# A decoder layer on one core: the feed-forward weights split before the value products, in other memory

## The chip, the core and the metric

The kernel runs on one core of a Trainium2 chip. Its work is done by TensorE (matmuls, PE in the profile, with the weight loads as PEld), VectorE (DVE), ScalarE (ACT) and GpSimd (POOL); SyncE (SP) issues the DMAs. The metric is the time of one execution in microseconds, as the median of several runs. One further execution is profiled; its own time stands beside its span.

## The reference

A post-norm decoder layer over `x` of 8 sequences of 128 tokens and 512 features:

```python
x = layernorm(x + attn(x))            # 32 query heads, 8 key/value heads of 128, int4 weights with scales, rope, causal
x = layernorm(x + xattn(x, ctx))      # 16 heads of 32; softmax over axis 0 (batch and heads)
x = layernorm(x + ffn(x))

def xattn(q, v, k):
    Q, K, V = (proj(t, W, b) for t, W, b in ((q, Wq, bq), (k, Wk, bk), (v, Wv, bv)))
    scores = einsum('bqd,bkd->bqk', Q, K) / sqrt(32)
    return einsum('bqk,bkd->bqd', softmax(scores, axis=0), V)      # heads put back as (d, head)

def ffn(x):                            # 8 experts, top 2, rank 16
    gates = relu(layernorm_affine(x @ gw1.T + gb1)) @ gw2.T + gb2
    w = ...                            # softmax of the top two, zero for experts over their capacity
    return x @ weight.T + einsum('enr,ero->no', einsum('ni,eir->enr', x, lora_A) * w.T[:, :, None], lora_B) / 16
```

## The kernel before

Products that need full fp32 accuracy are made of fp32r parts: an operand is rounded to a high part (a cast on ScalarE), the low part is the difference (a subtraction on VectorE or POOL), and three matmuls (high-high, high-low, low-high) are summed in PSUM. VectorE, ScalarE, POOL and TensorE each execute their instructions in the order in which the kernel writes them; SyncE's order is made by the framework.

The first 500 us are the self-attention. Then a string, `ORDER` (L57), sets the order of the second stage, one letter per step: among them `Q` (one of eight query products of the cross-attention, `queries`), `B` (score products), `M` and `E` (maxima and exponentials), `s` and `S` (sums of exponentials on POOL, L1038 to L1044; the last one is added up on TensorE, L1136), `z`, `Z` (the softmax denominator on TensorE, L1078) and `V` (a quarter of a value projection, L682, with the copy of the result at L687). Here `V` with `pxv` multiplies context parts by the split weights Wv. The scaled softmax factors are in `gmax`.

After `ORDER` the feed-forward weights `fw` (four pieces of 128x512) are loaded (L1161), the gate's small constants are made (`gate_constants`: memsets of `rank`, `ones`, `minus_one`, `places` and a row of `hT` on POOL, L1190 to L1198, and two VectorE instructions on `order`, L1196 and L1197, that read `rank`), and the identity is added to the weights' four diagonal blocks on POOL (L1205): that adds the residual to the product.

The third stage goes by sequences, i = 0 to 7. Strings `AV_FIRST` (i = 0 and 1, L79) and `AV_SEQ` give the order within a step: `A` value products with the probabilities (`cross_values`: TensorE `xav` L1384, copy to `avs` L1393), `B` transposes and residual (`cross_residual`: `tr_av` L1398, VectorE L1400, statistics with `rstd_x` and `nmr_x` on POOL at L252 and L254), `L` the normalisation of the previous sequence on ScalarE (L255), `X` its transposes with high and low parts `x2h`, `x2l` (`turn_x2`: L1240 to L1242), `P` the gate product `pg` (L1247), `f` one quarter of the queued work: first value projections, later the feed-forward product `pf` of the sequence before (L1261, three matmuls), and `W` one of four weighings of sequence i + 2: exponentials times factor and inverse denominator (L1234), on VectorE for three and on POOL for one (`WEIGH_ON`). With `B` of i = 1 come the late inverses (L1225 to L1227).

The split of the feed-forward weights lies in step i = 1, as letters `s` and `t`, since its memory is that of the split weights Wv, which the last value projection reads at the start of that step (`o`, `open_parts`):

```python
def split_weights(*kts):
    for kt in kts:
        nc.scalar.copy(fw_parts["h"][:, kt, :], fw[:, kt, :])
        nc.gpsimd.tensor_tensor(fw_parts["l"][:, kt, :], fw[:, kt, :], f32(fw_parts["h"][:, kt, :]), ALU.subtract)
```

A pool `fw` holds four rows (tag `raw`), used for `avs` and later for five of the eight output tiles `o`. The last stage (`END_SEQ`) finishes the gate, adds the experts' part and normalises.

Of the kernel before, what the change touches and what calls it, by code (L numbers as in the profile page):

```python
# [10 lines left out]
F32 = mybir.dt.float32  # L11
F32R = mybir.dt.float32r
# [41 lines left out]

ORDER = (  # L57
    'WXOOWXOOXAOKOTAAXOWOKTLKLKAOOTOOKWLOOTOOKLKXXQXKBKMAQKKKEBATQMLEKKVsAXVBAVTSsVQVTMSTLVEBVLNsLSQM'
    'EVBNQsVMEVBNVQSsSMgEVBQVNVsMEBVShMNsEVVVyVzSVZVVVV'
)  # L60
AV_SEQ = 'ALHfBNEJWWhhGffXKkfkPMWW'
GATES = ((0, 4, 'av'), (4, 2, 'sc'), (6, 1, 'po'), (7, 1, 'tr'))
# [13 lines left out]
SUB = (2, 3, 4, 5, 6)  # L76
TAIL = 8
TAIL_FIRST = 4
AV_FIRST = ('ALfBWWffWfW', 'AfLBffWWfoXsPWtW')  # L79
SEQUENCE = 'TpOpApOVpOpOp'  # L80
OUT_LANES = ('out0', 'out1')
TINY = 1e-25
# [51 lines left out]
def f32(ap):  # L134
    return ap.bitcast(F32)
# [3 lines left out]
def decoder_kernel(ctx: ExitStack, tc: tile.TileContext, a: dict, out: bass.AP):  # L139
# [37 lines left out]
    def pool(name, side="left", bufs=1):  # L177
        cm = tc.tile_pool(name=name, bufs=bufs, side=side)
        return cm, cm.__enter__()

    def close(cm):
        cm.__exit__(None, None, None)
# [889 lines left out]
    def sum_of(terms, first=True, last=True):  # L1072
# [4 lines left out]
        for i, x in enumerate(terms):  # L1077
            nc.tensor.matmul(ps[:], ident[:], x, start=first and i == 0, stop=last and i == len(terms) - 1)  # L1078

    last_terms = late_sum = None  # L1080
    for what in ORDER:
        n = count_of[what] = count_of.get(what, -1) + 1
        tick()
        if what == "O":
            outs.pop(0)()
            if not outs:
                flush()
                psum["ready"] += LANES.values()
        elif what == "K":
            late.pop(0)()  # L1090
        elif what == "V":
            open_exponentials()
            fill.pop(0)()
        elif what == "X":
            assert n < HALF or not outs
            norms.append(turn_out(n))
        elif what == "A":
            norms.pop(0)()
        elif what == "T":
            tokens.append(turn_x1(n))  # L1100
        elif what == "L":
            tokens.pop(0)()
        elif what == "Q":
            queries(n)
        elif what == "B":
            products(n)
        elif what == "M":
            if n == 0:
                open_maximum()
            group_maximum(n)  # L1110
        elif what == "W":
            wq_lows.pop(0)()
        elif what == "z":
            sum_of(last_terms[: 2 * HALF], last=False)
        elif what == "Z":
            nc.vector.tensor_tensor(gsum[:, 0, :], lsum[0][:], factor[:, 0, :], ALU.mult)
            nc.vector.tensor_tensor(gsum[:, 1, :], late_sum[:], factor[:, 1, :], ALU.mult)
            give(lsum[0], late_sum)
            sum_of(last_terms[2 * HALF :], first=False)
        elif what == "N":  # L1120
            last_chunk(SUB[n])
        elif what == "s":
            first_sum(n)
        elif what == "E":
            if n < GROUPS - 1:
                exponentials(n, range(3 if n in SUB else 4))
            else:
                last_terms = last_exponentials()
        elif what == "S":
            if n < EARLY:  # L1130
                group_sum(n)
            else:
                part = parts.pop(n)
                late_sum = bank("sum", "gsum6", (P, S))
                for i in range(HALF):
                    nc.tensor.matmul(late_sum[:], ident[:], part[:, i, :], start=(i == 0), stop=(i == HALF - 1))  # L1136
        elif what == "g":

            nc.gpsimd.tensor_tensor(
                gmax[:, early, :], gmax[:, early, :], across(gmax[:, EARLY - 1, :], EARLY - 1), ALU.subtract  # L1140
            )
            nc.scalar.activation(gmax[:, early, :], gmax[:, early, :], AF.Exp, scale=xscale)
        elif what == "h":
            nc.gpsimd.tensor_tensor(gsum[:, early, :], gsum[:, early, :], gmax[:, early, :], ALU.mult)
        elif what == "y":
            sum_of([gsum[:, i, :] for i in range(EARLY)])
    assert not (outs or late or norms or tokens or burst) and len(fill) == TAIL
    nc.vector.tensor_tensor(gmax[:, :KT, :], gmax[:, :KT, :], across(factor[:, 0, :], KT), ALU.mult)
    close(sub_cm)
    close(query_cm)  # L1150


    fw_cm, fwp = pool("fw", "right")
    fw = context_pool.tile([P, KT, D], F32, tag="ch", name="fw", bufs=2)
    fw_parts, x2 = {}, {}
    small = context_pool.tile([P, KT, D], F32, tag="cl", name="fg_lb", bufs=2)[:].rearrange("p k n -> p (k n)")
    fg = small[:, : KT * (FW - D)].rearrange("p (k c) -> p k c", k=KT)
    lb = small[:, KT * (FW - D) : KT * (FW - D) + D]

    for kt in range(KT):  # L1160
        nc.sync.dma_start(fw[:, kt, :], a["fw"][ts(kt, P), :D])  # L1161
    nc.sync.dma_start(fg, a["fw"][:, D:].rearrange("(k p) c -> p k c", p=P))
    nc.sync.dma_start(lb, a["loraB"])

# [33 lines left out]
        nc.gpsimd.memset(hT[GH : GH + 1], 1.0)  # L1198

    f_cm = open_ffn()  # L1200
    gate_constants()

    for kt in range(KT):
        diagonal = fw[:, kt, ts(kt, P)]
        nc.gpsimd.tensor_tensor(diagonal, diagonal, ident[:], ALU.add)  # L1205

    def split_weights(*kts):
        for kt in kts:
            nc.scalar.copy(fw_parts["h"][:, kt, :], fw[:, kt, :])
            nc.gpsimd.tensor_tensor(fw_parts["l"][:, kt, :], fw[:, kt, :], f32(fw_parts["h"][:, kt, :]), ALU.subtract)  # L1210


    inverse = gmax[:, GROUPS - 1, :]
# [152 lines left out]
    def engine_of(m, on=WEIGH_ON):  # L1366
        return nc.vector if on[m] == "v" else nc.gpsimd
# [10 lines left out]
    def cross_values(i):  # L1378

        av = bank("sc", f"xav{i}", (P, KT, S))  # L1380
        hf, j = divmod(i, HALF)
        for k in range(XH):
            m, g = divmod(k, 4)
            nc.tensor.matmul(  # L1384
                av[ts(g, XD), m, :],
                values_of(i)[:, ts(k, XD)],
                scores_of(4 * (hf * KT + m) + g)[:, j, :],
                start=True,
                stop=True,
                tile_position=(0, g * XD),  # L1390
            )
        avs[i] = fwp.tile([P, KT, S], F32, tag="raw", name=f"avs{i}", bufs=KT)
        nc.scalar.copy(avs[i][:], av[:])  # L1393

    def cross_residual(i):
        tr = bank("po", f"tr_av{i}", (P, KT, S))
# [24 lines left out]
    def step(what, i, state):  # L1421
        if what == "L" and i - 1 in apply:
            apply.pop(i - 1)()
        elif what == "W" and i + 2 < B:
            m = state["w"] = state.get("w", -1) + 1
            weigh(i + 2, m, engine_of(m))
        elif what == "A" and i < B:
            cross_values(i)
        elif what == "B" and i < B:
            cross_residual(i)  # L1430
            if i == 0:
                weigh(1, KT - 1, nc.vector)
            elif i == 1:
                late_inverses()
        elif what == "X" and i:
            turn_x2(i - 1)
        elif what == "P" and i:
            norm[i - 1] = gate_in(i - 1)
        elif what == "N" and norm:
            norm.pop(min(norm))()  # L1440
        elif (what == "G" and i == GATE_IN) or (what in "Hh" and i == GATE_IN + 1):
            gate(0, what)
        elif what == "M" and i == B - 1:
            apply.pop(i)()
        elif what == "k" and i == B - 1:
            gate(1, "h")
        elif what in "JK" and i == B - 1:
            gate(1, "GH"["JK".index(what)])
        elif what == "E" and i in EVACUATE:
            evacuate(EVACUATE.index(i))  # L1450
        elif what == "f" and fill:
            fill.pop(0)()
        elif what == "o":
            assert not fill
            open_parts()
        elif what in "st":
            split_weights(*((0, 1), (2, 3))["st".index(what)])

    def open_parts():

        fw_parts.update({m: xk["work"].tile([P, KT, D], F32R, tag=f"xwv{m}", name=f"fw{m}") for m in "hl"})
        x2.update({m: xk["work"].tile([P, HALF, KT, S], F32R, tag=f"c{m}1", name=f"x2{m}") for m in "hl"})

    rest = fill[TAIL_FIRST:]
# [65 lines left out]
    def finish(n):  # L1530
# [12 lines left out]
            aggregations.pop(0)()  # L1543

        if n % 3 == 0:
            o = fp.tile([P, D], F32, tag="x2f", name=f"o{t}", bufs=3)
        else:
            o = fwp.tile([P, D], F32, tag="raw", name=f"o{t}", bufs=KT)
        nmr = stat.tile([P, 1], F32, tag="nmr", name=f"nmr{t}")
        if APPLY_ON[n] == "p":  # L1550
            mine.append(lambda: nc.gpsimd.tensor_scalar(nmr[:], mv[:, 0:1], rstd[:], -1.0, ALU.mult, ALU.mult))
# [1 line left out]

        def apply():
            if APPLY_ON[n] == "v":
                nc.vector.tensor_scalar(o[:], y, mv[:, 0:1], rstd[:], ALU.subtract, ALU.mult)
            else:
                if APPLY_ON[n] == "a":
                    nc.vector.tensor_scalar(nmr[:], mv[:, 0:1], rstd[:], -1.0, ALU.mult, ALU.mult)
                nc.scalar.activation(o[:], y, AF.Identity, scale=rstd[:], bias=nmr[:])  # L1560
            nc.sync.dma_start(out[t], o[:])

        return apply

# [150 lines left out]
```

## Time and profile before

| | |
|---|---|
| median of 3 runs | 671.35 us (669.7 to 671.78) |
| profiled execution, its own time | 667.62 us |
| its span | 665.8 us |
| mean granted TensorE clock | 0.996 |
| busy: PE, PEld, DVE, ACT, POOL | 633.8, 491.1, 507.5, 481.1, 466.4 us |
| `fwl` low parts, L1210 | 2.54 us for two at 588.32, 3.39 us for two at 593.36 |

Times in the trace are microseconds from the span's start. A bracket at the end of a timeline row gives the idle time of the engine before it and what released it. The span ends 1.8 us short of the execution's own time; the sums of the prediction are made within the span.

### The profile page before, as it was taken

The page shows a single profiled execution, that of the slowest core. Times are in us where ns is not written, and L with a number is a line of the kernel's source. Part 1 is how long each engine was busy: PE and PEld are TensorE (multiplying, and loading weights), DVE is VectorE, ACT ScalarE, POOL GpSimd, SP SyncE. Part 2 cuts the span into 40 slices and gives each one's busy share as a digit, 9 for nine tenths or more (in the row PEclk, how much of TensorE's full clock was granted, in tenths as well). Part 3 has the DMA queues.
Part 4 walks back from the last instruction along what each step waited for, and adds up shares of the span by engine and source line. Part 5 has one row for each costly group of instructions (what it writes and reads, how often), then busy time and mean ns, then how long its engine had stood idle before and what let it go on. Part 6 is the DMA issues. An engine that isn't in the chain of part 4 may idle for free.

```text
span 665.8 us, 11531 instructions
## 1 busy us (share of the span) xinstructions
PE 633.8 (95%) x3514; PEld 491.1 (74%) x3514; DVE 507.5 (76%) x1314; ACT 481.1 (72%) x1213; POOL 466.4 (70%) x454
## 2 busy tenths in 40 slices
PE   6899999999999999999999999997999999979985
PEld 3786777777787787887777778875777877767762
DVE  4968767778787787787877878778676999977665
ACT  4376988998888888888889887786864664345433
POOL 4644978779797787978978788796832498475314
PEclk9999999999999999999999999999999999989999
DMA  8664433434244343334323342245300002000003
GB/s 292 168 180 122 120 87 81 100 91 111 71 100 103 77 109 98 79 92 106 93 70 79 78 129 64 50 124 199 136 1 1 1 1 100 1 1 1 1 1 127
DMA packets 31806, 57.38 MB, mean 86 GB/s; under 512 B 4862, under 2 KB 7166, under 8 KB 31744
## 3 DMA queue, kind: packets, MB, share of 16 engines
q1 hardware_dynamic: 31744, 56.64, 31.4%
q8 instruction: 28, 0.46, 0.3%
q14 instruction: 34, 0.28, 0.1%
HBM read 33.55 MB, written 2.10 MB: 54 GB/s over the span
## 4 chain that ended last, share of the span: by engine, by line
PE 71%; POOL 13%; DVE 5%; issue 4%; ACT 3%; DMA 2%; SPq 1%; POOLq 0%; DVEq 0%; ACTq 0%
PE ps L341 20%; PE po L483 15%; PE sc L408 7%; PE av L447 7%; PE tr L439 3%; PE pxk L718 3%; POOL sw L375 3%; POOL q L376 2%; PE pf L1261 2%; PE ps L327 2%; PE pxq L718 2%; PE pxv L682 2%; POOL t L374 2%; POOL part L1038 2%; POOL p L429 1%
## 5 line engine op out<-in xcount | busy, mean ns | idle before, releaser
L341 PE MATMUL ps<-xh,w 128*128 128x512 f32 x336 | 157.2, 468 | 1.9 <-ACT xv L331 1.6
L351 DVE SCALAR_TENSOR_TENSOR part<-ps,scales,part 128x512 f32<-128x512 f32 x168 | 125.7, 748 | 28.3 <-ACT part L347 18.4
L492 ACT ACTIVATE po<-po,ratios 128x512 f32<-128x512 f32 x174 | 112.5, 661 | 43.5 <-PE po L483 39.7
L341 PE MATMUL ps<-xl,w 128*128 128x512 f32 x336 | 132.5, 394 | 0.0
L374 POOL TENSOR_TENSOR t<-x,tables 128x512 f32<-128x512 f32 x70 | 90.2, 1288 | 41.0 <-DVE x L351 36.5
L483 PE MATMUL po<-ch,wo 128*128 128x512 f32 x256 | 112.5, 440 | 4.0 <-DVE po L490 2.6
L375 POOL TENSOR_TENSOR sw<-sw,tables 128x512 f32<-128x512 f32 x71 | 92.2, 1299 | 21.7 <-DMA sw<-x 20.0
L422 ACT ACTIVATE p<-p,nmx 128x128 f32<-128x128 f32 x256 | 99.1, 391 | 4.1 <-DVE nmx L413 4.1
L483 PE MATMUL po<-cl,wo 128*128 128x512 f32 x256 | 100.8, 394 | 0.0
L376 POOL TENSOR_TENSOR q<-t,sw 128x512 f32<-128x512 f32 x62 | 81.7, 1318 | 12.5 <-DVE sw L375 8.1
L341 PEld LDWEIGHTS ps<-xh,w 128*128 128x128 f32 x336 | 63.4, 189 | 20.9 <-PE po L483 6.5
L341 PEld LDWEIGHTS ps<-xl,w 128*128 128x128 f32 x336 | 63.7, 190 | 18.6 <-issue 10.1
L429 POOL TENSOR_TENSOR p<-p,rden 128x512 f32<-128x512 f32 x64 | 66.7, 1042 | 13.9 <-DVE rden L428 13.9
L408 PEld LDWEIGHTS sc<-k,q 128*128 128x128 f32 x512 | 67.3, 191 | 9.2 <-POOL q L376 3.7
L408 PE MATMUL sc<-k,q 128*128 128x128 f32 x512 | 68.5, 275 | 3.0 <-POOL q L376 2.8
L483 PEld LDWEIGHTS po<-ch,wo 128*128 128x128 f32 x256 | 48.1, 188 | 24.4 <-ACT po L492 6.0
L447 PE MATMUL av<-pt,v 128*128 128x512 f32 x128 | 65.5, 593 | 0.0
L413 DVE CUSTOM_DVE_ANT_0 p<-sc,causal 128x128 f32<-128x128 f32 x256 | 58.6, 286 | 7.0 <-PE sc L408 7.0
L351 DVE SCALAR_TENSOR_TENSOR x<-ps,scales,part 128x512 f32<-128x512 f32 x70 | 52.4, 749 | 14.7 <-PE ps L341 6.1
L347 ACT ACTIVATE part<-ps,scales 128x512 f32<-128x512 f32 x84 | 57.9, 689 | 0.0
L483 PEld LDWEIGHTS po<-cl,wo 128*128 128x128 f32 x256 | 48.3, 189 | 12.7 <-issue 4.5
L211 DVE TENSOR_TENSOR cl<-av,ch 128x512 fp32r<-128x512 f32 x64 | 44.1, 689 | 13.6 <-ACT ch L210 13.4
(266 smaller groups left out, 1306.2 us busy)
## 6 DMA issues: line engine op xcount, KB each, us to landing
sw<-x SPq DMA_DIRECT2D x160, 128.0 KB, 2.3
raw<-in_qkv SPq DMA_DIRECT2D x28, 384.0 KB, 3.1
oraw<-in_qw_o SPq DMA_DIRECT2D x32, 256.0 KB, 2.7
xraw<-in_xT SPq DMA_DIRECT2D x4, 512.0 KB, 5.6
ctxraw<-in_ctxT SPq DMA_DIRECT2D x2, 1024.0 KB, 5.1
acc<-in_x SPq DMA_DIRECT2D x8, 256.0 KB, 6.0
out<-o SPq DMA_DIRECT2D x8, 256.0 KB, 2.0
xwrawk<-in_WkT SPq DMA_DIRECT2D x1, 1024.0 KB, 5.4
```

The lines of the kernel that those rows point to most:

```text
L341: nc.tensor.matmul(ps[:], w[:, kt, ts(j, HD)], x[:, kt, ts(hf, HN)], start=(i == 0), stop=(i == 1))
L351: nc.vector.scalar_tensor_tensor(to, ps[:], sc, parts[0][:], ALU.mult, ALU.add)
L374: later(delay("cos"), lambda: engine("cos").tensor_tensor(seqs(t[:]), seqs(x[:]), table(cos_t[m]), ALU.mult), True)
L375: later(delay("sin"), lambda: engine("sin").tensor_tensor(seqs(sw[:]), seqs(sw[:]), table(sin_t[m]), ALU.mult), True)
L376: later(delay("q"), lambda: engine("q").tensor_tensor(dst, t[:], sw[:], ALU.add), True)
L408: nc.tensor.matmul(sc[:, r, :], t["q"][:, r, ts(j, S)], t["k"][:, ts(j, S)], start=True, stop=True)
L413: nc.vector.tensor_tensor_reduce(out=p[:, r, :], in0=sc[:, r, :], in1=causal[:], scale=-1.0, scalar=3e38, op0=ALU.add, op1=ALU.min, accum_ ...
L422: nc.scalar.activation(p[:, r, :], p[:, r, :], AF.Exp, scale=-1.0, bias=nmx[:, r : r + 1], accum_out=den[:, r : r + 1],)
L429: nc.gpsimd.tensor_tensor(p[:], p[:], rden[:].unsqueeze(2).to_broadcast([P, REP, S]), ALU.mult)
L447: nc.tensor.matmul(av[:], t["v"][:, j, :], pt[:], start=True, stop=True)
L483: nc.tensor.matmul(ps[:], o_w[g][:, r, ts(c, P)], t["c" + m][:, r, :], start=(r == 0 and i == 0), stop=(i == 1), skip_group_check=True,)
L492: later(delay("out"), lambda: nc.scalar.activation(ps[:], ps[:], AF.Copy, scale=sc))
```

## The change

The weights are loaded by a new letter `r` in `ORDER`, behind the last `Q`. A letter `c` behind the first `z` near the end of `ORDER` opens the memory of the parts, adds the four diagonals, makes the four high parts and the first two low parts. The high parts lie in a new pool in place of the former four rows, with the memory of the queries' weights given back before; the low parts lie in the memory of the second half of the cross-attention's keys (`kT1`). The other two low parts are made by `s` in step i = 0, behind `B`; the gate's constants by `q` at the end of step i = 0. One weighing of step i = 0 (`v`) moves from POOL to VectorE. Rows for `avs` and for five outputs are taken from the half of the cross-attention's queries, in `accT`, that isn't reused for exponentials.

```diff
-    'EVBNQsVMEVBNVQSsSMgEVBQVNVsMEBVShMNsEVVVyVzSVZVVVV'
+    'EVBNQsVMEVBNVQSsSMgEVBQrVNVsMEBVShMNsEVVVyVzcSVZVVVV'
-AV_FIRST = ('ALfBWWffWfW', 'AfLBffWWfoXsPWtW')
+AV_FIRST = ('ALfBsWWffvfWq', 'AfLBffWWfoXPWW')
+    def load_weights():
+        nonlocal fw
+        fw = context_pool.tile([P, KT, D], F32, tag="ch", name="fw", bufs=2)
+        for kt in range(KT):
+            nc.sync.dma_start(fw[:, kt, :], a["fw"][ts(kt, P), :D])
+    def open_weights():
+        nonlocal fw_cm
+        close(sub_cm)
+        close(query_cm)
+        fw_cm, pl = pool("fw", "right")
+        fw_parts["h"] = pl.tile([P, KT, D], F32R, name="fwh")
+        fw_parts["l"] = xk["kv"].tile([P, KT, D], F32R, tag="kT1", name="fwl")
+        for kt in range(KT):
+            diagonal = fw[:, kt, ts(kt, P)]
+            nc.gpsimd.tensor_tensor(diagonal, diagonal, ident[:], ALU.add)
+            nc.scalar.copy(fw_parts["h"][:, kt, :], fw[:, kt, :])
+    def low_weights(*kts):
+        for kt in kts:
+            nc.gpsimd.tensor_tensor(fw_parts["l"][:, kt, :], fw[:, kt, :], f32(fw_parts["h"][:, kt, :]), ALU.subtract)
+    def row():
+        kept[0] += 1
+        return qT[:, kept[0] % KT, ts(1, HN)]
+        elif what == "r":
+            load_weights()
+        elif what == "c":
+            open_weights()
+            low_weights(0, 1)
-    gate_constants()
-    for kt in range(KT):
-        diagonal = fw[:, kt, ts(kt, P)]
-        nc.gpsimd.tensor_tensor(diagonal, diagonal, ident[:], ALU.add)
-        avs[i] = fwp.tile([P, KT, S], F32, tag="raw", name=f"avs{i}", bufs=KT)
-        nc.scalar.copy(avs[i][:], av[:])
+        avs[i] = row().rearrange("p (m s) -> p m s", m=KT)
+        nc.scalar.copy(avs[i], av[:])
+        elif what == "v":
+            m = state["w"] = state["w"] + 1
+            weigh(i + 2, m, nc.vector)
-        elif what in "st":
-            split_weights(*((0, 1), (2, 3))["st".index(what)])
+        elif what == "s":
+            low_weights(2, 3)
+        elif what == "q":
+            gate_constants()
-        fw_parts.update({m: xk["work"].tile([P, KT, D], F32R, tag=f"xwv{m}", name=f"fw{m}") for m in "hl"})
-            o = fwp.tile([P, D], F32, tag="raw", name=f"o{t}", bufs=KT)
+            o = row()
```

More of the change, by code (lines that the diff above doesn't have):

```diff
@@ L1078, in sum_of @@
             nc.tensor.matmul(ps[:], ident[:], x, start=first and i == 0, stop=last and i == len(terms) - 1)
+    fw = fw_cm = None
+    fw_parts, kept = {}, [0]
+    def load_weights():
[20 more added lines that the diff above has]
+        return qT[:, kept[0] % KT, ts(1, HN)]
     last_terms = late_sum = None
@@ L1148, in decoder_kernel @@
     nc.vector.tensor_tensor(gmax[:, :KT, :], gmax[:, :KT, :], across(factor[:, 0, :], KT), ALU.mult)
[L1149 to L1155, printed above, removed]
+    assert fw_parts
+    x2 = {}
     small = context_pool.tile([P, KT, D], F32, tag="cl", name="fg_lb", bufs=2)[:].rearrange("p k n -> p (k n)")
@@ L1158, in decoder_kernel @@
     lb = small[:, KT * (FW - D) : KT * (FW - D) + D]
-    for kt in range(KT):
-        nc.sync.dma_start(fw[:, kt, :], a["fw"][ts(kt, P), :D])
     nc.sync.dma_start(fg, a["fw"][:, D:].rearrange("(k p) c -> p k c", p=P))
@@ L1200, in decoder_kernel @@
     f_cm = open_ffn()
-    gate_constants()
-    for kt in range(KT):
-        diagonal = fw[:, kt, ts(kt, P)]
[L1205 to L1210, printed above, removed]
     inverse = gmax[:, GROUPS - 1, :]
@@ L1545, in finish @@
         if n % 3 == 0:
-            o = fp.tile([P, D], F32, tag="x2f", name=f"o{t}", bufs=3)
+            o = fp.tile([P, D], F32, tag="x2f", name=f"o{t}", bufs=3)[:]
         else:
-            o = fwp.tile([P, D], F32, tag="raw", name=f"o{t}", bufs=KT)
+            o = row()
         nmr = stat.tile([P, 1], F32, tag="nmr", name=f"nmr{t}")
@@ L1555, in apply @@
             if APPLY_ON[n] == "v":
-                nc.vector.tensor_scalar(o[:], y, mv[:, 0:1], rstd[:], ALU.subtract, ALU.mult)
+                nc.vector.tensor_scalar(o, y, mv[:, 0:1], rstd[:], ALU.subtract, ALU.mult)
             else:
@@ L1559, in apply @@
                     nc.vector.tensor_scalar(nmr[:], mv[:, 0:1], rstd[:], -1.0, ALU.mult, ALU.mult)
-                nc.scalar.activation(o[:], y, AF.Identity, scale=rstd[:], bias=nmr[:])
-            nc.sync.dma_start(out[t], o[:])
+                nc.scalar.activation(o, y, AF.Identity, scale=rstd[:], bias=nmr[:])
+            nc.sync.dma_start(out[t], o)
         return apply
```

## The prediction

> **What bounds the kernel now.** The page's list of engines says that TensorE is busy for 95% of the span, so only its few idle places and slow places can be won. The chain that ended last lies on TensorE for 71% and on POOL for 13%. I then read the timelines of TensorE, POOL, VectorE and SyncE around the place where the feed-forward weights are split. TensorE's shows the one long stop (columns: start, duration, engine, line, operation, count, and in brackets the idle time and who ended it):
>
> ```profile
> 590.16 0.39 PE L1261 MATMUL pf<-fwh,x2l 128*128 128x512 f32 x1
> 591.73 0.40 PE L1261 MATMUL pf<-fwh,x2h 128*128 128x512 f32 x1
> 595.13 0.53 PE L1261 MATMUL pf<-fwl,x2h 128*128 128x512 f32 x1 [3.00 <-POOL fwl L1210]
> ```
>
> TensorE waits 3.00 us for the third low part of the weights. POOL's timeline tells why that part is late:
>
> ```profile
> 569.25 0.30 POOL L1190 MEMSET rank<- 128x1 f32 x8
> 569.85 0.94 POOL L1198 MEMSET tmp_hT<- 1x1024 f32 x1
> 570.88 2.12 POOL L1205 TENSOR_TENSOR fw<-fw,ident 128x128 f32<-128x128 f32 x4
> 582.11 1.34 POOL L254 TENSOR_SCALAR nmr_x<-mv_x,rstd_x 128x1 f32<-128x1 f32 x1
> 588.32 2.54 POOL L1210 TENSOR_TENSOR fwl<-fw,fwh 128x512 fp32r<-128x512 f32 x2 [0.66 <-ACT fwh L1209]
> 593.36 3.39 POOL L1210 TENSOR_TENSOR fwl<-fw,fwh 128x512 fp32r<-128x512 f32 x2
> ```
>
> The diagonals are ready at 573, but the split waits until the memory of Wv is free (last pxv at 585.74), and the last two lows stand behind POOL's share of the weighing. The VectorE rows used below:
>
> ```profile
> 571.36 0.48 DVE L1196 TENSOR_TENSOR order<-rank 128x64 f32<-128x64 f32 x1
> 573.82 0.29 DVE L1221 TENSOR_TENSOR gmax<-gmax 128x128 f32<-128x128 f32 x1
> 580.91 2.49 DVE L1234 TENSOR_TENSOR E<-E,gmax 128x512 f32<-128x512 f32 x4
> 583.86 0.69 DVE L1400 TENSOR_TENSOR acc<-acc,tr_av 128x512 f32<-128x512 f32 x1 [0.47 <-PE tr_av L1398]
> 587.76 0.69 DVE L1242 TENSOR_TENSOR x2l<-tr_x,x2h 128x512 fp32r<-128x512 f32 x1
> 589.72 1.69 DVE L1234 TENSOR_TENSOR E<-E,gmax 128x512 f32<-128x512 f32 x1
> ```
>
> The last row is one weighing that took 1.69 beside a POOL low part; four in a row take 2.49 alone, 0.60 from start to start. So the two engines hold each other up. Last, the table by stretches (duration, busy time of PE, PEld, DVE, ACT and POOL with counts, granted clock, DMA):
>
> ```profile
> 592.00:596.00 4.00, 1.00 (x4) 0.63 (x4) 3.52 (x6) 0.41 (x1) 4.00 (x4) 0.93 0.00 0
> 596.00:600.00 4.00, 4.00 (x32) 3.55 (x34) 0.69 (x1) 1.34 (x3) 1.53 (x3) 0.64 0.02 4
> ```
>
> After the stop the clock is granted at 0.64 until about 599, so the stop costs more than its 3.00.
>
> **The loads.** SyncE's timeline has the four weight loads at 557.72, directly behind the gate weights at 557.23 and just after the last query product (TensorE 557.04). In the changed program SyncE's order is the same: gate weights, weights, loraB. The loads were early already; this part of the change costs and brings nothing.
>
> **The first half of the split.** POOL's last sum ends at 569.30. What followed were memsets and the four diagonals, then idleness to 581. Now the diagonals and two lows follow at once; the memsets leave. VectorE has 0.30 of a halving left that waited for POOL, one more halving (0.30 alone) and a 0.68 product of the maxima to do in between. All in turn: 0.30 + 0.30 + 0.68 + 4 x 0.43 + 2 x 1.28 = 5.56, so POOL ends near 574.9. VectorE's first product with the inverses, at 573.82 so far, then waits for the second low: up to 1.0 (nothing, if the lows get through earlier). Behind it queue all weighings of the first two sequences, which release TensorE's value products: it idles 0.18 and 0.17 on them now. I take 0.9 on the path, near the upper end, since POOL's work is too long for the gap.
>
> [...]
>
> **ScalarE.** Its four casts (0.62 each) move from 587.6 to about 570 to 572.9, between two copies of values. The second copy slips from 571.49 to about 572.9; its bank is next taken by the gate product at 587.29, so cover of 14 us hides it. Without that cover 1.4 us. What leaves at 587.6 to 590 was hidden by the POOL lows.
>
> **The second half, and a new wait.** In the first step (i=0) VectorE takes a weighing over from POOL: five instead of four. POOL's order becomes: statistics of x0, lows 2 and 3, memsets. VectorE's two "order" instructions, which stood in a gap at 571.36, now come after the five weighings and wait for the rank memsets, that is behind both lows. Behind them on VectorE is queued the residual of sequence 1 and all that follows, x2l of sequence 0 included, which TensorE's third pf product needs. Step by step: the weighings start at 580.91 + 0.9 = 581.8 and end at 581.8 + 5 x 0.60 = 584.8; nmr_x, which ended with the last weighing in the trace too (583.45), ends at 584.9; lows 2.55 to 587.5; ranks 0.30 to 587.8; the two orders 0.89 (571.36 to 572.25) to 588.75; residual to epsilon 1.82 (583.86 to 585.68) to 590.55; late inverses and two weighings 2.0 (585.60 to 587.61) to 592.5; x2l 0.8 to 593.3. TensorE wants it at 590.16 + 0.9 = 591.05. So a stop of about 2.3 stands where one of 3.0 stood, 2 us further ahead in the work. The normalised sequence 1 (apply after nmr_x1, about 592.2 to 593.0) is then ready before its transposes. Left without the wait for ranks, x2l would come at about 589.9, before it is wanted. Lows, casts and constants themselves are then hidden by the earlier idle time of POOL.
>
> **The rest.** The rows of values and three of the eight outputs differ only in address: the copies keep their shape, the query half was last read by score products that ended at 561.1, and nothing new is waited for. Cost 0; with a hidden wait there, at most the 0.59 of one copy.
>
> **The sum.** From a third pf product to the next value product the undisturbed step takes 4.65 (601.20 to 605.85). So xav of sequence 3 starts at 593.35 + 4.65 = 598.0 instead of 599.62: 1.6 us less. After that both kernels run the same steps at full clock. 665.8 - 1.6 = 664.2 for the span; the profiled execution of 667.62 becomes 666.0. It lies 3.7 below the median of 671.35, so the same 1.6 off the median gives 669.7. With 0 for the first wait it is 2.5 less, with both lows contended at the 1.72 that the late ones took, 0.7 less.
>
> **Rivals.**
>
> *The clock keeps the gain (0.22).* Unslowed, the kernel before would go from 595.13 to xav in 3.02 (602.83 to 605.85): 598.15, only 0.15 after the changed one. So nearly the whole 1.6 is the lost clock. If the other stop of 2.3 slows the clock too, or if executions before are often not slowed, the gain is 0.1 to 0.2: 671.2. For it: a stop of 2.3 isn't much shorter. Against: the shorter stop has more work close around it, and the trace shows no slow clock after its other stops of up to 1.07. [...]
>
> *No stop at all (0.20).* If lows 2 and 3 slip in between the weighings without holding them, ranks come early and x2l by 591.05: xav at 591.05 + 4.65 = 595.7, 3.9 less: 667.5. For: POOL did slip its pow in between weighings (581.07 to 582.01). Against: nmr_x right after it couldn't.
>
> *VectorE becomes the bound (0.16), slower.* If nmr_x slips by 1 us to 585.9, each of lows 2 and 3 takes 1.72 and each following weighing 1.7 as at 589.72: lows to 589.4, ranks 589.7, orders 590.6, residual 592.5, inverses 0.8 and two weighings 3.4 to 596.7, x2l 597.5; xav at 597.5 + 4.65 = 602.2, 2.5 more: 673.9. It decides from x2l later than 595.0 (599.62 - 4.65) on. For: the rows exist. Against: POOL has little left to contend with after its memsets.
>
> **How the numbers follow.** The forecast's case gets 0.42, with a range of its own of 668.8 to 670.7. A measurement here can tell about 0.3%, 2.0 us. Of the forecast's 0.42 I put 0.19 beyond that; with "no stop" 0.39 faster. Within: 0.23 + 0.22 = 0.45. Slower 0.16. The range goes from 667.0, half a microsecond under "no stop", to 672.0, past the clock rival with a little of its spread; the slower case is left out.
>
> **What would show it.** Right: fwl rows at about 572 to 575 and 585 to 587.5, no stop at fwl, a stop of about 2.3 at pf<-x2l released by VectorE, orders at about 588 waiting for POOL rank, xav of sequence 0 up to 0.9 later, the clock 1.00 up to 600. Wrong: no stop at x2l (then faster), a stop over 4 us there (then slower), or a granted clock under 1 after it.

## The result and the profile after

The changed kernel takes 666.25 us (median of 11 runs, 663.99 to 668.04), the kernel before 669.54 (median of 11, 667.11 to 671.78): ratio 0.995, interval 0.9934 to 0.9966, so 3.3 us less. The profiled execution took 665.92, its span 664.1, at a mean granted clock of 0.997.

Up to the last sum of the second stage (`gsum` on TensorE: 569.36 before, 570.91 after) both programs give TensorE the same work, and executions of the same program already differ there by more than a microsecond (571.24 in the experiment `filled` below, which is the kernel before up to there). So times are compared from that sum on. The two rows of the kernel before:

```profile
569.36 1.16 PE L1136 MATMUL gsum<-part,ident 128*128 128x128 f32 x8
...
599.62 1.08 PE L1384 MATMUL xav<-E,xv 128*32 128x128 f32 x32
```

From the last sum to the value products (`xav`) of sequence 3 the kernel before needs 30.26 us, the changed one 27.00; to the end of the span 96.46 and 93.22. The two differences, 3.26 and 3.24, agree with the gain of the medians: everything lies ahead of sequence 3's value products.

TensorE's timeline of the changed kernel, as the prediction reads it (start, duration, engine, line, operation, count, idle time before it and who ended that):

```profile
570.91 1.16 PE L1169 MATMUL gsum<-part,ident 128*128 128x128 f32 x8
...
591.73 0.39 PE L1284 MATMUL pf<-fwl,x2h 128*128 128x512 f32 x1
593.18 0.50 PE L1284 MATMUL pf<-fwh,x2l 128*128 128x512 f32 x1 [1.06 <-DVE x2l L1265]
...
597.91 1.08 PE L1407 MATMUL xav<-E,xv 128*32 128x128 f32 x32
```

The stop for `fwl` is gone. In its place stands one for `x2l`, released by VectorE, as forecast; it is 1.06 long, not 2.3. POOL's timeline of the changed kernel:

```profile
570.82 2.52 POOL L1101 TENSOR_TENSOR fw<-fw,ident 128x128 f32<-128x128 f32 x4
573.30 2.53 POOL L1106 TENSOR_TENSOR fwl<-fw,fwh 128x512 fp32r<-128x512 f32 x2
...
583.91 1.35 POOL L255 TENSOR_SCALAR nmr_x<-mv_x,rstd_x 128x1 f32<-128x1 f32 x1
585.23 3.00 POOL L1106 TENSOR_TENSOR fwl<-fw,fwh 128x512 fp32r<-128x512 f32 x2
588.16 0.30 POOL L1223 MEMSET rank<- 128x1 f32 x8
```

The lows lie about where they were expected (counted from the last sum, the second pair ends 0.82 us earlier than forecast), and the ranks behind the second pair. VectorE's timeline:

```profile
575.35 0.63 DVE L1244 TENSOR_TENSOR gmax<-gmax 128x128 f32<-128x128 f32 x1
...
582.73 3.09 DVE L1257 TENSOR_TENSOR E<-E,gmax 128x512 f32<-128x512 f32 x5
588.50 0.23 DVE L1229 TENSOR_TENSOR order<-rank 128x64 f32<-128x64 f32 x1 [2.69 <-POOL rank L1223]
588.64 0.22 DVE L1230 TENSOR_TENSOR order<-rank 128x64 f32<-128x64 f32 x1
588.78 0.68 DVE L1423 TENSOR_TENSOR acc<-acc,tr_av 128x512 f32<-128x512 f32 x1
...
592.44 0.68 DVE L1265 TENSOR_TENSOR x2l<-tr_x,x2h 128x512 fp32r<-128x512 f32 x1
```

VectorE stands idle for 2.69 us ahead of its first order: that is the new wait. The product with the inverses (first row) took 0.63, where 0.29 stood before: that is the wait for the second low (one_low, below, takes it away). Last, the table by stretches (duration, busy time of PE, PEld, DVE, ACT and POOL with counts, granted clock, DMA):

```profile
592.00:596.00 4.00, 2.94 (x17) 2.42 (x17) 3.83 (x10) 1.35 (x4) 2.53 (x4) 1.00 0.02 4
596.00:600.00 4.00, 4.00 (x49) 2.90 (x48) 3.51 (x9) 2.27 (x5) 2.40 (x4) 1.00 0.00 0
```

Behind the stop the clock stays at 1.00, where it was granted at 0.64 before (at one half for 3.41 us, from 595.45 on).

### The profile page after: what moved, and what is told of

Its sections match the earlier page's. It is cut to its first block, busy times and chain, and to the rows that moved or that the text cites. A ratio compares the mean times of both kernels' runs of the same rounds, so it can differ in the third digit from the quotient of the medians.

```text
span 664.1 us, 11534 instructions
## 1 busy us (share of the span) xinstructions
PE 632.3 (95%) x3514; PEld 489.4 (74%) x3514; DVE 506.1 (76%) x1315; ACT 481.6 (73%) x1213; POOL 465.2 (70%) x453
## 4 chain that ended last, share of the span: by engine, by line
PE 68%; POOL 13%; DVE 7%; issue 5%; ACT 3%; DMA 3%; SPq 1%; POOLq 0%; DVEq 0%; ACTq 0%
PE ps L342 19%; PE po L484 15%; PE sc L409 7%; PE av L448 6%; PE pxk L719 3%; PE tr L440 3%; POOL sw L376 3%; PE pf L1284 2%; POOL q L377 2%; PE ps L328 2%; PE pxq L719 2%; DMA sw<-x 2%; POOL t L375 2%; POOL part L1039 2%; POOL p L430 1%
```

## The experiments

All times in the first column are of the profiled execution, from its last sum to sequence 3's value products. "Stop" is TensorE's, at the product named. Ratios are against the kernel before on the same chip: late_split, filled, w_pool and ranks_early ran on one (its median there 669.65), the other four experiments on another (669.53).

| kernel | to xav, us | stop | clock behind it | ratio, interval |
|---|---|---|---|---|
| before | 30.26 | 3.00 `fwl` | half for 3.4 us | |
| changed | 27.00 | 1.06 `x2l` | 1.00 | 0.995 (0.9934 to 0.9966) |
| late_split | 30.24 | 3.00 `fwl` | half for 3.4 us | 1.0001 (0.9987 to 1.0015) |
| filled | 29.25 | 0.33 and 0.29 `fwl` | 1.00 | 0.9981 (0.9967 to 0.9995) |
| w_pool | 29.33 | 1.80 `x2l` | half for 3.4 us | 0.9968 (0.9949 to 0.9988) |
| ranks_early | 26.43 | 0.47 `x2l` | 1.00 | 0.9925 (0.9906 to 0.9943) |
| w_pool_filled | 27.76 | 0.19 `x2l` | 1.00 | 0.9945 (0.9926 to 0.9964) |
| orders_late | 25.72 | none | 1.00 | 0.993 (0.9915 to 0.9945) |
| one_low | 25.39 | none | 1.00 | 0.9913 (0.9897 to 0.9928) |
| changed_again | 27.00 | 1.04 `x2l` | 1.00 | 0.994 (0.9925 to 0.9954) |

Executions of one kernel spread over some 4 us, and in some of them the clock is halved for 3.41 us at about 34 us from the start (of the profiled ones in those of w_pool_filled, orders_late and changed_again, granted at 0.50 there); the first column is free of that. The code differences below are shortened, and the comments in them aren't in the kernels.

### late_split: the loads, the memory and the rows, without the earlier split

```diff
-AV_FIRST = ('ALfBsWWffvfWq', 'AfLBffWWfoXPWW')
+AV_FIRST = ('ALfBWWffWfW', 'AfLBffWWfoXsPWtW')
             open_weights()      # now opens the memory only
-            low_weights(0, 1)
+    gate_constants()            # and the diagonals, at their former place
+        elif what in "st":      # high and low parts of two pieces each, in step 1
```

> The changed kernel's memory (parts in the queries' weights and the keys, rows in the queries), but the parts made where the kernel before made them, all four weighings and constants at their old places. Theory A (the time comes from when the parts are made): TensorE's stop at the low part is back at about 3.0 us, the ratio to before is 1.000 within 0.002. Rival B (the memory and the rows bring the time): the ratio stays at 0.995.

TensorE's timeline of this kernel:

```profile
595.56 0.50 PE L1284 MATMUL pf<-fwl,x2h 128*128 128x512 f32 x1 [3.00 <-POOL fwl L1103]
```

The stop is back at 3.00, the clock halves for 3.41 us (596.15 to 599.56) and the time is that of before. Loads, memory and rows cost and bring nothing, as the prediction had it. All of the gain comes from where the instructions of the split, of the constants and of the one weighing stand, since this kernel puts all three back.

### filled: the kernel before, with the stop filled by spare products

Twelve products into a PSUM bank that is free then, ahead of the one that waits for the third low part; the wait itself stays.

```diff
+FILL = 12
+                if t == 0 and kt == 2 and i == 1:
+                    spare = banks.tile([P, 512], F32, tag=psum["named"]["pc"], name="spare")
+                    for _ in range(FILL):
+                        nc.tensor.matmul(spare[:], x2["h"][:, 0, 0, :], fw_parts["h"][:, 0, :], start=True, stop=True)
```

> The kernel before with 12 extra products (512 columns, 2.8 us at full clock) into a PSUM bank that is free then, queued on TensorE right before the product that stopped 3.0 us for the low part; they add nothing to the output. Theory C (half or more of the gain is the clock that slows after the stop): the stop is filled, its end stays, the clock stays at 1.00 up to 600, value products of sequence 3 start 1.2 to 1.5 us earlier after the last sum than in the profile before (30.26 us), ratio about 0.998. Rival D (the gain is all the length of the stop): no change, ratio 1.000, or 0.3 us slower where the extra products run past the end of the wait.

TensorE's timeline, and the table by stretches:

```profile
593.83 2.89 PE L1265 MATMUL spare<-fwh,x2h 128*128 128x512 f32 x12
597.05 0.50 PE L1266 MATMUL pf<-fwl,x2h 128*128 128x512 f32 x1 [0.33 <-POOL fwl L1211]
...
598.74 0.50 PE L1266 MATMUL pf<-fwl,x2h 128*128 128x512 f32 x1 [0.29 <-POOL fwl L1211]
```

```profile
598.00:602.00 4.00, 3.71 (x48) 2.90 (x46) 1.63 (x6) 1.70 (x4) 1.59 (x4) 1.00 0.02 4
```

The weights' parts come as late as before, yet the clock stays at 1.00 and sequence 3's value products come 1.01 earlier, the median 1.24. The expectation's 1.2 to 1.5 left out the last row: at full clock TensorE also catches up with the fourth low part and waits 0.29 for it. So of the change's 3.26 some 1.0 is the clock, and 2.25 (29.25 to 27.00) is the shorter wait itself, net of the first wait's 0.3.

### w_pool and w_pool_filled: the weighing back on POOL, then its stop filled

```diff
-AV_FIRST = ('ALfBsWWffvfWq', 'AfLBffWWfoXPWW')
+AV_FIRST = ('ALfBsWWffWfWq', 'AfLBffWWfoXPWW')
```

> The changed kernel with the third weighing of step 0 on POOL again, as before. Theory E: VectorE is done 0.6 us earlier, but POOL puts a weighing of 1.28 us between the lows and the ranks for which VectorE waits: the stop at x2l grows from 1.06 to about 1.8 us, ratio to before 0.996. Rival F (five weighings on VectorE make x2l late): the stop shrinks to about 0.5 us, ratio 0.994.

TensorE's timeline, and the table by stretches:

```profile
594.08 0.51 PE L1284 MATMUL pf<-fwh,x2l 128*128 128x512 f32 x1 [1.80 <-DVE x2l L1265]
```

```profile
591.51:594.92 3.41, 1.61 (x13) 1.06 (x9) 3.27 (x11) 1.40 (x2) 1.81 (x3) 1.00 0.00 0
...
595.00:598.40 3.40, 3.40 (x12) 2.72 (x11) 3.30 (x7) 0.41 (x1) 3.23 (x4) 0.51 0.03 5
```

The stop grew to 1.80 since the weighing stands on POOL ahead of the ranks. But sequence 3's value products came 2.33 later than in the changed kernel, three times the 0.74 by which the stop grew: the clock was halved behind this stop. Whether that is the whole rest, the next kernel asks, with seven spare products in the same stop:

```diff
+FILL = 7
+                if t == 0 and kt == 0 and i == 2:
+                    spare = banks.tile([P, 512], F32, tag=psum["named"]["pc"], name="spare")
+                    for _ in range(FILL):
+                        nc.tensor.matmul(spare[:], x2["h"][:, 0, 0, :], fw_parts["h"][:, 0, :], start=True, stop=True)
```

> The kernel with the third weighing on POOL, and 7 extra products (512 columns, 1.6 us) into a free bank on TensorE right before the product that stops 1.80 us for x2l there; they add nothing to the output. Theory C (its profiled execution lost 1.3 to 1.6 us to a clock that was halved for 3.41 us after that stop of 1.80): the stop's end stays, the clock stays at 1.00 there, value products of sequence 3 start at about 27.9 us after the last sum instead of 29.33, median at 0.996 or below where the unfilled one had 0.997. Rival G (those 1.5 us come from POOL and VectorE being late, not from the clock): 29.3 us again.

```profile
593.22 1.78 PE L1288 MATMUL spare<-fwh,x2h 128*128 128x512 f32 x7
595.20 0.50 PE L1289 MATMUL pf<-fwh,x2l 128*128 128x512 f32 x1 [0.19 <-DVE x2l L1266]
```

`x2l` comes no earlier, TensorE stays busy, the clock there is 1.00, and the value products come at 27.76: 1.57 less than in w_pool. The remaining 0.76 to the changed kernel is the length of the stop (1.80 less 1.06 is 0.74). So in the profiled executions the weighing on VectorE brings 0.76 by itself and another 1.57 because the clock isn't halved. The ratios over all runs (0.9968 and 0.9945) point the same way, but their intervals overlap.

### ranks_early: the ranks ahead of the lows

```diff
+    gate_constants()            # the memsets alone, directly behind open_ffn()
         elif what == "q":
-            gate_constants()
+            gate_orders()       # VectorE's two orders, where they were
```

> The changed kernel with its memsets (rank, ones and so on) directly behind the first two lows on POOL, which is idle there, and only the two order instructions on VectorE at the end of step 0. Theory E (the 1.06 us stop at x2l in the changed kernel comes from VectorE waiting 2.69 us for the ranks behind the lows): the stop vanishes, residual of sequence 1 about 2.3 us earlier, value products of sequence 3 at 25.9 us after the last sum instead of 27.0, ratio to before about 0.9935. Rival F (VectorE's five weighings and POOL's lows make x2l late anyway): a stop over 0.5 us stays there, ratio 0.995.

VectorE's timeline of this kernel, then POOL's:

```profile
585.28 1.32 DVE L1232 TENSOR_TENSOR order<-rank 128x64 f32<-128x64 f32 x1
586.52 1.32 DVE L1233 TENSOR_TENSOR order<-rank 128x64 f32<-128x64 f32 x1
587.76 0.67 DVE L1426 TENSOR_TENSOR acc<-acc,tr_av 128x512 f32<-128x512 f32 x1
```

```profile
584.77 2.99 POOL L1106 TENSOR_TENSOR fwl<-fw,fwh 128x512 fp32r<-128x512 f32 x2
```

The orders wait for nothing now, but each takes 1.32 instead of 0.23, and the second ends 0.08 after POOL's lows. The residual of sequence 1 starts 17.31 after the last sum (17.87 in the changed kernel): 0.56 earlier, not 2.3. The stop falls to 0.47, not to nothing. The semaphore was only part of what held VectorE: beside the lows each order lasted about as long as a low by itself (1.28 in one_low, 2.53 for two here at 572.85).

### orders_late: the orders behind step 1 as well

```diff
-AV_FIRST = ('ALfBsWWffvfWq', 'AfLBffWWfoXPWW')
+AV_FIRST = ('ALfBsWWffvfW', 'AfLBffWWfoXPWWq')
```

(on top of ranks_early)

> The changed kernel with early ranks and with the two order instructions on VectorE moved from the end of step 0 to the end of step 1, where POOL has no low parts to make. Theory H (what was left of the stop, 0.47 us with early ranks, comes from the two orders, which read two operands in SBUF and took 1.32 us each beside the lows): residual of sequence 1 starts 2.4 us earlier, no stop over 0.1 us at x2l, value products of sequence 3 at 25.9 to 26.0 us after the last sum instead of 26.43. Rival F (VectorE's five weighings make x2l late): the stop stays at about 0.5.

VectorE's timeline:

```profile
586.62 0.68 DVE L1426 TENSOR_TENSOR acc<-acc,tr_av 128x512 f32<-128x512 f32 x1
...
590.90 0.68 DVE L1268 TENSOR_TENSOR x2l<-tr_x,x2h 128x512 fp32r<-128x512 f32 x1
```

The residual follows the weighings at once, 14.83 after the last sum (2.48 earlier than in ranks_early), and the stop is gone. That tells the orders' place from everything else in the queue. The medians don't tell the two kernels apart: the intervals of their ratios overlap, and the profiled 0.71 (26.43 to 25.72) is less than they resolve.

### one_low: only one low ahead of the value products

```diff
         elif what == "c":
             open_weights()
-            low_weights(0, 1)
+            low_weights(0)
         elif what == "s":
-            low_weights(2, 3)
+            low_weights(1, 2, 3)
```

(on top of orders_late)

> The kernel with early ranks and late orders, and with one low part instead of two before the value products; three are made after the statistics of sequence 0. Theory I (the second low part holds up the first product with the inverses by 0.34 us, and that delay reaches TensorE): value products of sequence 0 end 0.3 us earlier after the last sum, those of sequence 3 start at about 25.6 us; ratio to before 0.991 to 0.992. Rival J (three lows in a row on POOL meet the late inverses and weighings and make x2l or the third weight part late): a stop of 0.3 us or more at x2l or a low part, no gain over two lows.

VectorE's timeline:

```profile
574.26 0.29 DVE L1247 TENSOR_TENSOR gmax<-gmax 128x128 f32<-128x128 f32 x1
...
586.04 0.92 DVE L1251 TENSOR_TENSOR gmax<-factor,gmax 128x128 f32<-128x128 f32 x1
586.99 1.24 DVE L1252 TENSOR_TENSOR gmax<-gmax 128x128 f32<-128x128 f32 x1
...
589.56 0.68 DVE L1268 TENSOR_TENSOR x2l<-tr_x,x2h 128x512 fp32r<-128x512 f32 x1
```

The first wait, small as it was, was real: the product with the inverses is back at 0.29 and the value products of sequence 3 come 0.33 earlier. The price that the rival theory named shows too (two late inverses at 0.92 and 1.24; 0.28 and 0.29 in the changed kernel, 0.90 and 0.29 in orders_late), and is hidden: `x2l` is still in time. Median 663.62, 5.9 us under the kernel before and 2.0 under the changed one on the same chip (665.61). All its six runs (up to 664.94) lie below all five of the changed kernel (from 665.05). Its ratio is the lowest here, though the interval overlaps those of ranks_early and orders_late, and by a hair that of changed_again.

### changed_again: the changed kernel unaltered, beside these

> The changed kernel itself, unaltered, to have its ratio beside the others on the same chip. Every theory: 0.995 within 0.002, value products of sequence 3 at 27.0 us after the last sum where the clock is not halved before them.

27.00 to the value products and a stop of 1.04, as in the first profile: the first column repeats to a few hundredths.

## Why the prediction missed the size

**Right.** Loads and rows at nothing (late_split: 1.0001). ScalarE's casts at nothing: counted from the last sum the second copy of values slips by 0.86, and TensorE waits for the same 0.73 before the gate product in both profiles. The path: no stop at `fwl`, a new one at `x2l`, made by the orders' wait for ranks behind POOL's lows (2.69 idle; orders_late takes it away). A direction of faster. The clock at 1.00 behind the stop came true by luck: the stop was shorter than the one for which it was forecast (see the rivals).

**Wrong: the size.** 669.7 was forecast and 666.25 measured, 3.45 less and below the range. Two terms make that up: the base, and a gain whose waits were priced too high.

The base is 1.81 of it: the forecast took its 1.6 off a median of three runs (671.35), where eleven runs give 669.54 and the 29 runs beside the first four experiments 669.65. The range, too, was built down from those three. That the profiled execution took 665.92 where 666.0 was forecast is luck: it came to its last sum 1.55 us later than the profiled one before, which hides half of the gain.

The gain is the other 1.64: 1.62 forecast (30.26 to 28.64), 3.26 measured from the last sum. Set from there, the forecast's own chain stands beside the trace so (the last column has what each step adds to the gain over the forecast):

| step of the sum | forecast, us | measured | |
|---|---|---|---|
| first of the five weighings starts | 12.44 | 11.82 | 0.62 more |
| `nmr_x` ends | 15.54 | 14.35 | 0.57 more |
| lows 2 and 3 end | 18.14 | 17.32 | 0.37 of it lost |
| residual of sequence 1 starts | 19.39 | 17.87 | 0.70 more |
| `pf` product that waits for `x2l` starts | 23.99 | 22.27 | 0.20 more |
| value products of sequence 3 start | 28.64 | 27.00 | 0.08 lost |

- *The first wait* was put at 0.9, "near the upper end", from all of POOL's and VectorE's instructions taken in turn; it was 0.34 (0.63 less 0.29). VectorE stood idle for 1.34 ahead of the reciprocal, waiting for the denominator from TensorE, and POOL went on in that time.
- *`nmr_x`* was said to end with the last weighing, as in the one row of before. It takes 1.35 there as before, but a fifth weighing follows it now: it ended 0.56 ahead of that weighing's end.
- *The lows* took 3.00 instead of 2.55, since their first 0.59 lies under that last weighing (2.54 in w_pool, which has no fifth weighing there). Besides the 0.08 of the last row this term alone erred to the other side.
- *The orders* were priced at 0.89 from the row at 571.36, where they stood beside POOL's diagonals (570.88 to 573.00): that row is in part waiting for POOL. With POOL at memsets they take 0.23 and 0.22, 0.14 from start to start.
- *Without the wait for ranks*, the prediction said, `x2l` would come before it is wanted. ranks_early removes that wait and a stop of 0.47 is left: the prediction had left out that the orders would lie beside the lows, where they took 1.32 each.

**The rivals.** *The clock keeps the gain* fell in its price: it had the kernel before, unslowed, only 0.15 behind the changed one, while filled shows 2.25. Of the 2.10 that this is off, 1.64 is the gain above; the other 0.46 (29.25 against its 28.79) is nearly all the wait for the fourth low (0.29 idle, 0.45 later than in an undisturbed step), which its 3.02 us taken from a later step doesn't hold. Part of its mechanism stands: some 1.0 of the gain is the clock. The prediction set against it that the clock stayed after other stops of up to 1.07; the trace of before has longer ones without a slow clock, 1.76 ahead of 32.97 and 1.62 ahead of 56.76. Yet behind w_pool's stop of 1.80 the clock was halved, and a stop of 2.3 with the clock at 1.00 behind it, as forecast, is in no profile here once the products of 512 columns have come down from 0.63 to 0.40 us each (at about 15 us in the trace of before). The changed kernel's stop of 1.06 left it at 1.00; the last section has what was measured ahead of and behind such stops. *No stop at all* came nearest, 667.5 (a gain of 3.9), though a stop was there: its condition didn't hold, and early ranks alone leave 0.47 (ranks_early); the orders have to leave as well. *VectorE becomes the bound* needed `nmr_x` to slip and each weighing behind the residual to take 1.7; neither happened, the two behind the late inverses taking 1.28 together.

## What to carry to other kernels

Before a busy row is used as the price of an instruction that moves, see what the other engine did in that row: the same 128x64 instruction took 0.22, 0.48 or 1.32 us here by what POOL was doing. When a step moves, look for what else waits in the queue behind it: most of what the change left on the table (1.28 of 1.61 us to the value products, orders_late and one_low) hung on two tiny instructions in front of the critical one. Measure a stop in two parts, its length and the clock behind it, by filling it with spare products; and measure the kernel before often enough that its median is known better than the gain.

## What the runs showed of the hardware

That the clock is halved behind w_pool's stop of 1.80 was not expected. In the kernel before it is granted at half from 595.45 to 598.87. The 3.41 us ahead of that read so, and after them a stretch of the same length that holds the changed kernel's stop:

```profile
592.04:595.45 3.41, 0.41 (x2) 0.30 (x2) 3.33 (x5) 0.41 (x1) 3.41 (x4) 1.00 0.00 0
```

```profile
591.45:594.87 3.42, 2.36 (x12) 1.69 (x12) 3.32 (x9) 1.40 (x2) 2.04 (x2) 1.00 0.02 5
```

0.41 us of matmul, and the clock behind it was granted at half; 2.36, and it stayed at 1.00. w_pool's 1.61 (shown above) was followed by half, and late_split's 0.59 (592.74 to 596.15).

The length of a stop alone doesn't decide in these executions. Just ahead of 33 us from the start TensorE stands still for 1.74 to 1.86 us in all ten, and only three have a halved stretch behind it: changed_again, w_pool_filled and orders_late, each with 1.55 us of matmul in the 3.41 us ahead (31.01 to 34.42, 30.80 to 34.21 and 30.44 to 33.85). Nor does that amount of matmul decide alone: late_split has 1.60 from 29.54 to 32.95 and one_low 1.59 from 29.76 to 33.17, and the clock stayed at 1.00 behind both. What tells these stops apart is not shown by the runs. All of this was read off afterwards and not tried by itself, and the ends of matmuls in a trace are modelled, so the amounts are known no better than that.
